# A decoder layer: second norm and feed-forward bias per tile among the gates, projection pieces in column tiles, preparation work spread

## The chip, the cores and the metric

The kernel runs on one core of a Trainium2 chip. The metric is the device time of one execution in microseconds (us). The kernel before was timed three times: 2485.95, 2486.40 and 2489.06 us, median 2486.4. A core has five engines with their own instruction queues, each strictly in order for our purpose: TensorE (PE; its weight loads are listed apart as PEld), VectorE (DVE), ScalarE (ACT), GpSimd (POOL) and SyncE (SP), which here only issues DMAs.

## The reference

One decoder layer in float32 on x of shape 4 x 1024 x 512 (batch, token, feature):

```python
x = layernorm(x + attn(x))          # 32 heads of 16; q, k, v each through two linear layers
x = layernorm(x + gates(x, ctx))    # a causal convolution of two taps, then a gated cell
x = layernorm(x + ffn(x))           # 8 bit quantised input, weights -1, 0, 1, bias

# attn: q = lin(lin(x, wq), vq), the same for k and v; softmax(q k / 4) v; lin(o, wo)
# gates: out = ctx + conv(x) + bias, split in four along 2048 channels (it, ot, gt, ft)
#   ct = sigmoid(ft) * previous_c + sigmoid(it) * tanh(gt);  ht = sigmoid(ot) * tanh(ct)
#   the result is ht and ct, one after the other
# ffn: clip(round(x / scale), -127, 127) * scale, times (ternary_weight - 1), + bias
```

In the gates the tokens of a batch are the channels (1024 = 512 of h and 512 of c) and the 512 features are the sequence.

## The kernel before, in words

**Attention** (`attention`, to line 723). A unit is four heads of one batch, 32 units in all, `u`. Each unit has two passes over its scores: `nat` (L449) computes them with queries in the partitions, and DVE takes their maximum (L465, negated), which is written as a row into the operands of the second pass; `scores` (L519) computes them again, transposed, ACT takes the exponentials (L530), and `weigh` (L545) multiplies by v. `nat` of unit u + 1 runs along with `scores` of unit u. These matmuls contract over 32 rows, so four of them stand in the array side by side as row tiles (the profile writes 32*128); the weighing has 32 output rows for each head, and four heads stand as column tiles (128*32).

The loop runs over 32 steps `h`. Each step issues one `nat` and one `scores`; on every fourth (h % 4 == 1) comes one weighing, on every fourth (h % 4 == 3) one piece of `fill` (or of `out_pieces`): a projection of q or k of a later pair of units in 176 or 160 columns (`project`, L383), a piece of v (`project_v`, L408) or of the output projection (`out_piece`, through `Handed.project`, L222) in 256 columns. These pieces use the full array (128*128): four matmuls that add up over 512 features. A float32 matmul shows as two records. Ahead of the first unit twelve q and k pieces and five `fold_v` pieces (L398) stand next to each other; the last unit has 16 steps without `nat`, with a weighing and an out piece on every second one.

Four `stages` normalise a unit's output: read the denominators (`den`), take reciprocals (L578), spread them (`rbc`), multiply on POOL (`o_n`, L592) and write to HBM. They run at steps 5, 9, 13 and 20 of the next unit. All order in the kernel is the order in which the instructions are written; nothing reorders them within an engine.

Some work for the tail is issued from within: at unit 24, step 5, the loads of the out weights and of the rest (`load_rest`); at step 21 `prepare_rest` turns the ternary weights into floats (L204, POOL) and makes the quantisation scale (L208 to L214, DVE); at unit 30, step 5, `first_norm(0)` begins with `norm_stats` (means L98, square root L107 on ACT, reciprocal L108).

**Tail** (`tail`). A small planner holds later work: `after(n, work)` puts it at the end of the n-th `step()` from there. There is one step for each gate, each out projection tile and each feed-forward tile. Two rounds, for batches (0, 2) and (1, 3). A round has 4 token tiles x 2 batches x 4 gates. A gate (`gate`) is 32 matmuls of 171 columns (64 records; `pc` for two taps, `pa` for two, L792), then four DVE operations (L796 to L802) that add them to the ctx tile `u`, and an ACT function (L803). The convolution uses a fast scheme over three columns, which needs the sum and the difference of the two weight taps (`sum_taps`, L161, POOL) and sums of x (`fir_parts`, L176 to L182, DVE, into `xf`). After a tile's four gates `combine` does six operations on POOL and a Tanh on ACT (L814 to L822), and two bn_stats on DVE (L826, L827). PSUM has two buffers each for `pc`, `pa`, the feed-forward's sum and the transposes.

`second_norm` then normalises a whole batch (L98, L107, L108, L116). Feed-forward takes 16 tiles a round: `quantise` (ACT L862, DVE L863, L864), `turn` (four transposes L870, ACT copy L872), `feed` (L878), `ff_bias` (L909), `residual` (L883, L884), and `third_norm` in groups with the write of the output. `quantise` runs three tiles ahead, `turn` one. Between the rounds `project_out` does the out projection of batches 1 and 3 (L222, 512 columns).

Of the kernel before, what the change touches and what calls it, by code (L numbers as in the profile page):

```python
# [29 lines left out]
def decoder_kernel(ctx: ExitStack, tc: tile.TileContext, a, out):  # L30
# [18 lines left out]
    with ExitStack() as rest:  # L49
        tail(rest, tc, a, out, ident, eps, hand)  # L50


class Handed:
# [47 lines left out]
    def deviations(self, mv, pool, name, t0=0, n=NT):  # L101

        nc = self.nc
        rstd = pool.tile(
            [P, NT], F32, tag="rstd", bufs=1 if pool is self.shared else 3, name=f"rstd{name}_{t0}"
        )
        nc.scalar.activation(rstd[:, t0 : t0 + n], mv[:, t0 : t0 + n, 1], AF.Sqrt, bias=self.eps, scale=1.0)  # L107
        nc.vector.reciprocal(rstd[:, t0 : t0 + n], rstd[:, t0 : t0 + n])  # L108
        return rstd

    def norm_stats(self, stats, pool, name):
        mv = self.means(stats, pool, name)
        return mv, self.deviations(mv, pool, name)
# [6 lines left out]
    def first_norm(self, b):  # L120
# [3 lines left out]

        def deviations():
            made.extend(self.norm_stats(self.stats[b], self.shared, f"1_{b}"))

        def part(t0):
            if t0 == 0:
                self.nc.vector.tensor_copy(x1[:, :, 0], self.z0[:, b, :])  # L130
            for t in (t0, t0 + 1):
                self.normalised(x1[:, t, 1 : D + 1], self.y[b][:, t, :], *made, t)

        return x1, [deviations] + [lambda t0=t0: part(t0) for t0 in range(0, NT, 2)]

    def load_ctx(self, k, pool):
# [4 lines left out]
        u = (pool if k % 2 else self.shared).tile([P, 4, D + 1], F32, tag="u", name=f"u{b}_{t}")  # L141
# [16 lines left out]
    def sum_taps(self, w):  # L158
        for tap, op in ((2, ALU.add), (3, ALU.subtract)):
            for i in range(FT):  # L160
                self.nc.gpsimd.tensor_tensor(w[:, i, tap, :], w[:, i, 0, :], w[:, i, 1, :], op)  # L161
# [39 lines left out]

    def prepare_rest(self):
        nc = self.nc
        nc.gpsimd.tensor_scalar_add(self.w_f, self.w_f.bitcast(mybir.dt.int32), -1.0)  # L204
# [12 lines left out]
    def project(self, b, t, cols, pt, bias=False):  # L217
# [3 lines left out]
        for f in range(FT):  # L221
            nc.tensor.matmul(  # L222
                pt, attn_t[:, f, t * P : (t + 1) * P], self.w_o[:, f, cols], start=f == 0, stop=f == FT - 1
            )
# [8 lines left out]
def attention(ctx, tc, a, attn_d, ident, shared, hand):  # L233
# [8 lines left out]
    b_v = const.tile([P, D], F32, tag="b_v", name="b_v")  # L242
# [37 lines left out]
    for i in range(2):  # L280
        t = once.tile([P, 32], F32, tag=f"neg{i}", name=f"neg{i}")
        nc.gpsimd.memset(t, 0.0)
        negs.append(t)
    for i in range(2):
# [734 lines left out]
```

## Time and profile before

| what | value |
|---|---|
| median of the runs shown | 2486.4 us |
| profiled execution, its own time | 2487.75 us |
| its span, first to last instruction | 2486.0 us |
| mean granted TensorE clock | 0.996 |
| attention, to the first gate | 1974.58 us |
| first gates and feed-forward, to the first out projection | to 2203.64 us |
| second gates | from 2258.57 us |
| last feed-forward matmul, last DVE instruction | about 2478.3, 2482.97 us |

The page gives each engine's busy time, the chain of work that ended last (followed backward from the last instruction through whatever released each step), and groups of instructions by line with their mean time. A line in order of time reads: start, duration, engine, line and operation, output <- input, shape, count of records, and in brackets the engine's idle time before it with what ended it. Idle time of an engine costs only where the chain passes through it.

### The profile page before, as it was taken

What the parts mean: (1) busy time and instruction counts of PE and PEld (TensorE: products, weight loads), DVE (VectorE), ACT (ScalarE), POOL (GpSimd) and SP (SyncE); (2) the same over time, 40 slices, a digit from 0 to 9 for tenths busy, and PEclk for the clock granted to TensorE, in tenths of its full rate; (3) what the DMA queues carried; (4) which work ended last, traced back from release to release, by engine and by line L of the source; (5) the groups of instructions that cost most, each with busy time, mean ns of one, the idle gap of its engine ahead of it and who ended that gap; (6) DMA issues with size and microseconds to landing.
All of it is one profiled execution on the core that took longest, in us unless ns stands there. A gap on an engine that the chain in (4) does not pass through costs nothing.

```text
span 2486.0 us, 60152 instructions
## 1 busy us (share of the span) xinstructions
PE 2452.5 (99%) x25492; PEld 1781.1 (72%) x25492; DVE 1748.6 (70%) x2198; ACT 1306.5 (53%) x2558; POOL 333.5 (13%) x275
## 2 busy tenths in 40 slices
PE   9999999999999999999999999999999999999998
PEld 6677777777777777777777776677776799547984
DVE  3767777777777777777777777777777465888568
ACT  1166666666666666666666666666655511411132
POOL 2000000000000000000000002000020265311640
PEclk9999999999999999999999999999999999999999
DMA  6101111111110211101111114110120243240311
GB/s 216 48 11 20 20 25 54 21 23 22 23 26 16 58 21 20 21 20 23 22 21 21 24 20 134 21 24 16 25 79 11 66 157 136 84 153 18 119 35 68
DMA packets 80653, 120.80 MB, mean 49 GB/s; under 512 B 39056, under 2 KB 39056, under 8 KB 80384
## 3 DMA queue, kind: packets, MB, share of 16 engines
q1 hardware_dynamic: 79808, 115.90, 16.5%
q8 instruction: 201, 3.29, 0.6%
q10 hardware_dynamic: 576, 1.05, 0.1%
q14 instruction: 68, 0.56, 0.1%
HBM read 80.77 MB, written 18.35 MB: 40 GB/s over the span
## 4 chain that ended last, share of the span: by engine, by line
PE 91%; DVE 5%; POOL 2%; DMA 0%; ACT 0%; issue 0%; SPq 0%; DVEq 0%; POOLq 0%
PE nat L449 22%; PE av L545 19%; PE st L519 18%; PE proj L383 10%; PE v L408 5%; PE po L222 5%; PE pa L792 5%; PE pc L792 5%; PE fold L344 1%; PE pf L878 1%; POOL w L161 1%; DVE y L116 1%; DVE y L883 1%; DVE y L909 1%; DVE xq L864 1%; DVE stats L884 1%
## 5 line engine op out<-in xcount | busy, mean ns | idle before, releaser
L465 DVE TENSOR_REDUCE mx<-nat 128x2 f32<-128x1024 f32 x1008 | 1187.7, 1219 | 453.2 <-PE st L519 424.4
L530 ACT ACTIVATE at<-st 128x512 f32<-128x512 f32 x2016 | 1042.4, 603 | 625.5 <-PE st L519 610.0
L449 PE MATMUL nat<-qk 32*128 32x512 f32 x4032 | 1013.3, 614 | 3.8 <-DVE mx L465 3.8
L519 PE MATMUL st<-qk 32*128 32x256 f32 x8064 | 999.2, 387 | 0.0
L519 PEld LDWEIGHTS st<-qk 32*128 32x128 f32 x8064 | 656.0, 184 | 45.7 <-issue 3.1
L545 PE MATMUL av<-at,v_sb 128*32 128x256 f32 x8192 | 498.8, 382 | 0.6 <-ACT at L530 0.6
L449 PEld LDWEIGHTS nat<-qk 32*128 32x128 f32 x4032 | 343.3, 184 | 174.1 <-DVE mx L465 120.3
L545 PEld LDWEIGHTS av<-at,v_sb 128*32 128x32 f32 x8192 | 241.3, 110 | 223.4 <-ACT at L530 90.5
L592 POOL TENSOR_TENSOR o_n<-o_sb,rbc 128x512 f32<-128x512 f32 x64 | 96.1, 1523 | 1694.3 <-DMA rbc<-rec_d 1233.9
L383 PE MATMUL proj<-xT,w_qk 128*128 128x176 f32 (+1 forms) x1536 | 270.2, 320 | 0.7 <-ACT w_qk L349 0.7
L383 PEld LDWEIGHTS proj<-xT,w_qk 128*128 128x128 f32 x1536 | 223.7, 189 | 64.6 <-ACT at L530 60.0
L792 PE MATMUL pc<-xf,w 128*128 128x171 f32 x1024 | 161.9, 310 | 6.0 <-DVE u L796 4.4
L792 PE MATMUL pa<-xf,w 128*128 128x171 f32 x1024 | 161.4, 310 | 0.0
L792 PEld LDWEIGHTS pc<-xf,w 128*128 128x128 f32 x1024 | 153.6, 191 | 7.7 <-DVE u L796 4.9
L792 PEld LDWEIGHTS pa<-xf,w 128*128 128x128 f32 x1024 | 153.7, 191 | 0.0
L803 ACT ACTIVATE u<-u,b_c 128x512 f32<-128x512 f32 x64 | 45.5, 720 | 170.7 <-DVE u L802 170.7
L408 PE MATMUL v<-w_v,xT 128*128 128x256 f32 x512 | 126.0, 391 | 0.0
L222 PE MATMUL po<-w_o,big 128*128 128x256 f32 (+1 forms) x384 | 118.9, 459 | 2.1 <-ACT at L530 2.1
L878 PE MATMUL pf<-w_f,xq_t 128*128 128x512 f32 x256 | 117.2, 602 | 3.8 <-DVE y L883 2.3
L408 PEld LDWEIGHTS v<-w_v,xT 128*128 128x128 f32 x512 | 92.5, 189 | 34.4 <-ACT at L530 16.6
L222 PEld LDWEIGHTS po<-w_o,big 128*128 128x128 f32 x384 | 70.3, 190 | 49.2 <-issue 31.6
L558 DVE TENSOR_TENSOR o_sb<-av,o_sb 128x256 f32<-128x256 f32 x128 | 54.3, 424 | 72.0 <-PE av L545 71.5
(97 smaller groups left out, 1213.2 us busy)
## 6 DMA issues: line engine op xcount, KB each, us to landing
qk<-qk SPq DMA_DIRECT2D x256, 64.0 KB
w<-in_conv_wT SPq DMA_DIRECT2D x32, 512.0 KB
u<-in_ctx SPq DMA_DIRECT2D x16, 1024.0 KB
xT<-in_xT SPq DMA_DIRECT2D x16, 512.0 KB
rbc<-rec_d SPq DMA_DIRECT2D x128, 64.0 KB
attn<-o_n SPq DMA_DIRECT2D x256, 32.0 KB
big<-attn SPq DMA_DIRECT2D x4, 2048.0 KB
y<-in_x SPq DMA_DIRECT2D x4, 2048.0 KB
```

The lines of the kernel that those rows point to most:

```text
L222: nc.tensor.matmul(pt, attn_t[:, f, t * P : (t + 1) * P], self.w_o[:, f, cols], start=f == 0, stop=f == FT - 1)
L383: nc.tensor.matmul(pt[:, 0:n], w[:, f, gg * P : (gg + 1) * P], xts[b][:, f, cols], start=f == 0, stop=f == FT - 1)
L408: nc.tensor.matmul(pt, xts[b][:, f, t * P : (t + 1) * P], w_v[:, f, cols], start=f == 0, stop=f == FT - 1)
L449: nc.tensor.matmul(pts[n], q_ts[u % 4][r : r + 32, qt * P : (qt + 1) * P], k_ts[u % 4][r : r + 32, kh * 512 : kh * 512 + 512], start=True, ...
L465: nc.vector.tensor_reduce(mxs[u][:, qt, 2 * pair : 2 * pair + 2, kh], pt, AX.X, ALU.max, negate=True)
L519: nc.tensor.matmul(st[:, k * QW : k * QW + QW], k_ts[u % 4][r : r + 32, kt * P : (kt + 1) * P], q_ts[u % 4][r : r + 32, qq * QW : qq * QW ...
L530: nc.scalar.activation(at, st, AF.Exp, scale=0.25)
L545: nc.tensor.matmul(av[32 * j : 32 * j + 32, :], v_sb[b % 2][:, kt, c * VW : c * VW + 32], ats[u, 2 * i + n // 2, j][:, n % 2 * QW : n % 2 ...
L558: nc.vector.tensor_add(o, av, o)
L592: nc.gpsimd.tensor_mul(o_n[:, :, half * 256 : half * 256 + 256], o_sb[:, cols].rearrange("p (s e) -> p e s", e=2), rbc[:, cols].rearrange( ...
L792: nc.tensor.matmul(pt, w[:, i, tap, o : o + P], xf[:, tap, i, :], start=i == 0, stop=i == FT - 1)
L878: nc.tensor.matmul(pt, xq_ts[b, t][:, f, :], hand.w_f[:, f, :], start=f == 0, stop=f == FT - 1)
```

## The change

1. `by_quarters`: the q, k, v, fold and out pieces of attention are issued as four column tiles of 32 output rows each, for each of the four contraction steps (16 matmuls where there were 4). The out projection in the tail stays as it was.
2. `prepare_w_f` in four parts at step 21 of units 25 to 28; the scale at step 21 of unit 29 (`prepare_rest`).
3. `first_norm` has its means apart from its square root, and the reciprocal is issued with the first normalised part. At unit 30 only the means are issued; the parts of the last unit begin a step earlier. At the end of attention the last unit's reciprocals stand between the two halves of `first_norm(2)`.
4. The sums of weights come in quarters, after steps 3, 6, 6 and 7; those for the second round at its start.
5. The second norm is done for each pair of tiles (h and c) in `combine`, as steps 3 to 6; the last of them adds the feed-forward's bias on POOL, into the place of x1 that is no longer needed. `residual` adds from there; `ff_bias` and `second_norm` go. The first three tiles are quantised after the first three of the last four gates.
6. Feed-forward goes through the tiles in the order 0, 1, 2, 4, 5, 6, 3, 7; its very last tile is done in two halves of 256 columns; statistics are kept in order of work; the third norm's groups and their steps differ.
7. Memory: ctx tiles share two slots in `shared`, both loaded in the last unit; `rbc` has a pool of its own; `b_v` shares the slot of `b_f`; batch 3's attention is loaded after step 9 of the first feed-forward in place of step 1.

```diff
+def by_quarters(nc, pt, lhsT, rhs):
+    for f in range(FT):
+        for j in range(4):
+            r = slice(32 * j, 32 * j + 32)
+            nc.tensor.matmul(pt[r, :], lhsT(f)[:, r], rhs(f), start=f == 0, stop=f == FT - 1)
...
     def deviations(self, mv, pool, name, t0=0, n=NT):
...
-        nc.scalar.activation(rstd[:, t0 : t0 + n], mv[:, t0 : t0 + n, 1], AF.Sqrt, bias=self.eps, scale=1.0)
-        nc.vector.reciprocal(rstd[:, t0 : t0 + n], rstd[:, t0 : t0 + n])
-        return rstd
+        part = rstd[:, t0 : t0 + n]
+        nc.scalar.activation(part, mv[:, t0 : t0 + n, 1], AF.Sqrt, bias=self.eps, scale=1.0)
+        return rstd, lambda: nc.vector.reciprocal(part, part)
...
-    def sum_taps(self, w):
+    def sum_taps(self, w, i):
         for tap, op in ((2, ALU.add), (3, ALU.subtract)):
-            for i in range(FT):
-                self.nc.gpsimd.tensor_tensor(w[:, i, tap, :], w[:, i, 0, :], w[:, i, 1, :], op)
+            self.nc.gpsimd.tensor_tensor(w[:, i, tap, :], w[:, i, 0, :], w[:, i, 1, :], op)
...
+    def prepare_w_f(self, f):
+        w = self.w_f[:, f, :]
+        self.nc.gpsimd.tensor_scalar_add(w, w.bitcast(mybir.dt.int32), -1.0)
...
         pt = ps_st.tile([P, QW], F32, tag="st", name=f"proj{p}_{which}_{t0}")
-        for f in range(FT):
-            nc.tensor.matmul(
-                pt[:, 0:n], w[:, f, gg * P : (gg + 1) * P], xts[b][:, f, cols], start=f == 0, stop=f == FT - 1
-            )
+        by_quarters(nc, pt[:, 0:n], lambda f: w[:, f, gg * P : (gg + 1) * P], lambda f: xts[b][:, f, cols])
...
-                if u >= 0 and i > 2 and firsts:
+                if u >= 0 and i > 1 and firsts:
                     firsts.pop(0)()
...
-                if i == 3 and u >= 0:
-                    hand.load_ctx(0, None)
-                if i == 10 and u >= 0:
-                    hand.sum_taps(hand.first_w)
+                if i in (3, 5) and u >= 0:
+                    hand.load_ctx(i // 2 - 1)
+                if i in (8, 9, 10, 11) and u >= 0:
+                    hand.sum_taps(hand.first_w, i - 8)
...
-                if h == 21 and u == 24:
+                if h == 21 and 25 <= u < 29:
+                    hand.prepare_w_f(u - 25)
+                if h == 21 and u == 29:
                     hand.prepare_rest()
...
     hand.x1[2], parts = hand.first_norm(2)
-    for part in parts:
+    for part in parts[:2]:
+        part()
+    stages.pop(0)()
+    for part in parts[2:]:
         part()
...
+    def combine(b, t, k):
+        u, y, x = us[b, t], ys2[b], x1[b]
         ig, og, gg, fg = (u[:, i, 0:D] for i in range(4))
+        both = (t, 4 + t)
+        made = []
...
         def third():
-            nc.vector.bn_stats(stats2[b][:, 4 + t, :], y[:, 4 + t, :])
-            nc.vector.bn_stats(stats2[b][:, t, :], y[:, t, :])
-        after(2 if last else 1, second)
-        after(4 if last else 3, third)
...
+            for n, tt in enumerate(both):
+                nc.vector.bn_stats(stats2[b][:, 2 * t + n, :], y[:, tt, :])
+            made.append(hand.means(stats2[b], stat, f"2_{b}", 2 * t, 2))
+        def fourth():
+            made.extend(hand.deviations(made[0], stat, f"2_{b}", 2 * t, 2))
+        def fifth():
+            mv, rstd, invert = made
+            invert()
+            for n, tt in enumerate(both):
+                hand.normalised(y[:, tt, :], y[:, tt, :], mv, rstd, 2 * t + n)
+        def sixth():
+            for tt in both:
+                nc.gpsimd.tensor_add(x[:, tt, 0:D], y[:, tt, :], b_f)
+        for n, work in ((1, second), (3, third), (4, fourth), (5, fifth), (6, sixth)):
+            after(n, work)
...
+    def residual(b, n, t, pt, cols=slice(0, D), half=0):
+        x2 = ys2[b][:, t, cols]
+        nc.vector.tensor_add(x2, pt, x1[b][:, t, cols])
+        nc.vector.bn_stats(stats3[b][:, n + half, :], x2)
...
+            if (b, n) == (B - 1, NT - 1):
+                for half in range(2):
+                    cols = slice(half * 256, half * 256 + 256)
+                    pt = feed(b, t, cols)
+                    residual(b, n, t, pt, cols, half)
...
+            group = {5: 2, 6: 1, 7: 1}.get(n, 4 if n == 3 else 0) if last else 4 * (n % 4 == 3)
             if group:
-                third_norm(b, t + 1 - group, group, end > 3)
+                first, invert, parts = third_norm(b, n + 1 - group, group)
+                first()
+                if group == 4:
+                    after(1, invert)
+                    for m, part in enumerate(parts):
+                        after(1 + m, part)
...
-                    gate(b, t, g, w, (lambda: [turn(batches[0], tt) for tt in (0, 1)]) if last else None)
+                    gate(b, t, g, w, (lambda: [turn(batches[0], order[m]) for m in (0, 1)]) if last else None)
                     if g == 3:
-                        combine(b, t, k, last)
-                        if t == 3 and b == batches[0]:
-                            after(3, lambda b=b: second_norm(b, True))
+                        combine(b, t, k)
+                    if t == 3 and b == batches[1] and g < 3:
+                        quantise(batches[0], order[g])
                     if b == batches[0] and g == 0 and (n, t) != (1, 3):
                         w_next = hand.load_conv(4 * n + t + 1, wp)
-                        after(3, lambda w=w_next: hand.sum_taps(w))
+                        if t < 3:
+                            for i, m in enumerate((3, 6, 6, 7)):
+                                after(m, lambda w=w_next, i=i: hand.sum_taps(w, i))
...
-            after(1, lambda: hand.load_attention(3, hand.shared.tile([P, NT * (D + 1)], F32, tag="big0", name="big3")))
+            after(9, lambda: hand.load_attention(3, big3()))
```

## The prediction

> **What bounds the kernel.** I read the page's engine shares first, then the chain that ended last, then the order of time in the places where the chain leaves TensorE.
>
> ```profile
> PE 2452.5 (99%) x25492; PEld 1781.1 (72%) x25492; DVE 1748.6 (70%) x2198; ACT 1306.5 (53%) x2558; POOL 333.5 (13%) x275
> PE 91%; DVE 5%; POOL 2%; DMA 0%; ACT 0%; issue 0%; SPq 0%; DVEq 0%; POOLq 0%
> ```
>
> TensorE is busy 99% and is 91% of the chain. So time is won in two ways only: TensorE's own work gets shorter, or one of its few waits goes. For the first, the order of time on TensorE in a steady attention unit:
>
> ```profile
> 624.55 1.93 PE L545 MATMUL av<-at,v_sb 128*32 128x256 f32 x32
> 626.42 0.70 PE L449 MATMUL nat<-qk 32*128 32x512 f32 x2
> ...
> 628.35 1.99 PE L408 MATMUL v<-w_v,xT 128*128 128x256 f32 x8
> 630.28 0.70 PE L449 MATMUL nat<-qk 32*128 32x512 f32 x2
> ```
>
> Both pieces stream 256 columns eight times (a float32 matmul is two records). The weighing, in four column tiles (128*32), takes 626.42 - 624.55 = 1.87 us from its start to the next block's; the full-array piece takes 1.93. At single records it is 1.864 and 1.924. The difference is at the head: the first weights take 186 ns to load for 128 columns, 106 for 32, and the second pass starts 320 ns after the first in a v piece, 240 in a weighing. The quarters give 20 ns back, since the fourth starts 20 ns after the first.
>
> The waits, in order of time:
>
> ```profile
> 1546.56 5.38 POOL L204 TENSOR_SCALAR w_f<-w_f 128x2048 f32<-128x2048 int32 x1
> 1546.91 3.31 DVE L213 TENSOR_TENSOR sc<-sc 128x1 f32<-128x1 f32 x1
> 1551.47 0.70 PE L449 MATMUL nat<-qk 32*128 32x512 f32 x2 [3.35 <-DVE mx L465]
> 1877.34 1.99 PE L222 MATMUL po<-w_o,big 128*128 128x256 f32 x8 [2.12 <-ACT at L530]
> 1990.74 2.60 PE L792 MATMUL pc<-xf,w 128*128 128x171 f32 x16 [1.89 <-DVE u L796]
> 2016.83 4.24 PE L792 MATMUL pc<-xf,w 128*128 128x171 f32 x16 [2.50 <-DVE u L796]
> 2131.05 0.66 PE L870 MATMUL tr<-ident,xq 128*128 128x128 f32 x4 [2.64 <-DVE xq L864]
> 2142.36 0.63 PE L870 MATMUL tr<-ident,xq 128*128 128x128 f32 x4 [2.37 <-DVE xq L864]
> ```
>
> The brackets are TensorE's idle time. 4.24 us for 16 records that take 2.5 elsewhere is half the clock. The view by stretches (TensorE, its loads, DVE, ACT, POOL; the last three are granted clock, DMA share, GB/s) has it after the first gap too:
>
> ```profile
> 1550.00:1612.00 62.00, 60.53 (x716) 42.61 (x720) 44.51 (x48) 37.04 (x74) 4.89 (x3) 0.97 0.11 21
> ```
>
> 0.97 of 62 us is 3.4 us at half, at most 1.7 us lost; so after the gaps of 3.35, 2.50, 2.64 and 2.37, not after 2.12.
>
> **A. Quarters.** Between two row-tiled blocks stand 178 projection pieces, 58 of v, 25 of out and one fold, each with the same head: 262 x 0.060 = 15.7 us. Seven further out pieces of the last unit follow a weighing directly; both become column tiles, and the change of tiling between them (about 0.09 us of spacing and 0.10 of exposed weight load) goes: 7 x 0.20 = 1.4. The pieces ahead of the first unit stand next to each other and gain nothing. **17.1 us**, all on the path, since each unit repeats at 57.84 us with DVE at 71% and ACT at 64%. Below: 13, if a third of the head stays with 160 and 176 columns, which no column tile of the trace has.
>
> A rule of the Trainium skill speaks against it ("TensorE: Matmul & The Clock Gate", the section on 56 against 53.3 ns): a matmul has an issue floor of about 25 ns, or about 62 ns when the instructions are decoded by the sequencer. Four quarters at 62 are 248 ns a pass, where a projection's pass takes 150 (176 columns) or 136 (160): some 150 us lost over all pieces. The weighing's row decides: four records a pass of 216 ns, 54 each, so 62 does not hold here. The 25 would cost nothing (4 x 25 is under 136). The trace shows single starts 7 ns apart but no sustained rate under 54 ns; the pieces need 34 to 37. I take the floor as not binding; the rest is a rival below.
>
> **B. Preparation of the rest.** The outputs' spacing shows the loss in that unit: v at 1503.66, which plus 57.84 minus 7.65 (the pair's distance) is 1553.85, and the piece comes at 1559.14: 5.29 us. The cause is DVE's scale operations (1x1 tensor-tensor, 0.14 us alone, up to 3.31 beside GpSimd's 5.38), with eight reductions queued behind. Now GpSimd's operation is four of some 1.35 us, one per unit, and the scale is made at unit 29, step 21. There GpSimd's adds and o_n end at 1835.5, and step 21 falls at about 1839, so seven operations cost DVE some 1.1 us, against slack of about 1.4 per reduction pair. I take 0.3 us left: **5.0** (3 to 5.3).
>
> **C. First norm at unit 30.** Table load 1.28, sqrt 0.30, table load 1.28 hold ACT 2.9 us and DVE's reciprocal 1.92. They move to the last unit, step 2, where ACT waits anyway (weighing and out piece give 3.6 us of TensorE work in between): **2.1** (0 to 2.1).
>
> **D. Start of the tail to the end of the first feed-forward**: 1974.58 to 2203.64 = 229.1 us. TensorE's own work: 32 gates x 4.67 = 149.3, two turns 0.9, feed-forward 14 x 3.87 + 2 x 3.44 = 61.1. The excess is 17.8. What goes: the 1.89 (rbc has its own pool, so the new xf no longer waits for o_n), the 2.50 with its slow clock (DVE's L827 waited for POOL behind eight sums of taps, 9.92 us; they come in quarters after steps 3, 6, 6, 7, so combine starts with its gate), and the 6 us in which feed-forward was DVE's (4.1 to 4.8 us a tile; minus the 0.69 of ff_bias and the second norm's 0.5, under 3.87). GpSimd gets 2 x 1.2 more per tile pair: 2 x (7.1 + 2.4) + 10 = 29 of 37.3 us, which fits.
>
> What comes: reciprocal L578 now stands ahead of the eight L116, and den lands about 1.5 us after its last issue (as rec_d does), so DVE is 2.7 us later; the third gate's PSUM needs it only at 1984.0, covered by 1.3 us. In the last four gates each quantise waits behind its gate's ACT (0.72 + 0.81), and stands ahead of DVE's next gate. Following the queues from gate 4's end: DVE 2.0, first xq 6.1 (GpSimd beside it stretches L863/L864 to 1.3 each, as at 2140), gate 5 done 8.6, second xq 11.0, bn_stats 12.4, gate 6 14.9, its ACT and identity 16.4, sqrt with a table load 18.0, copies of the transposes from there: the first feed has its operand at 18.6, where TensorE is at 14.9. Without the stretch it is 1.8 us late. I take 2.8, and 1.0 for the clock. The Tanh of the last combine stands ahead of the fourth quantise (second is no longer put off): another 2.2. New: 149.3 + 0.9 + 2.8 + 1.0 + 61.1 + 2.2 = 217.3, gain **11.8** (5 to 17).
>
> Here a second rule weighs: "ScalarE: Activation LUTs", what a table load costs: 1283 ns and a drain of 1380 for each switch. The trace has 1.28 and 0.30, and the next load at once, 2.9 a pair. Sixteen norms now switch among the gates; at 2.9 a pair stays inside a gate's 4.67 us. At the page's 5.3 it would not, and the copies at both ends would be 1.4 later: 2.8 us in all. I take the row.
>
> **E. Second round**: gates from 2258.57, last feed until 2478.26 = 219.7. It waited less (0.97 from xf, 0.71 and 0.2 at the turn). New: 217.3 + 0.97 = 218.2: **1.5** (-4 to 6.5).
>
> **F. The end**: from the last matmul to the span's end 7.7 us, 2 of them DVE's lag. New: half an add 0.43, stats 0.4, means 0.2, sqrt and reciprocal 0.8, L116 0.55, write 3.0 = 5.5: **2.2** (1 to 3).
>
> **At nothing**, and what hides it: the second ctx tile's 1 MB leaves at step 5 of the last unit, not on SP ahead of the weights' issue at 1992.24 (gain up to 0.4 in a queue with 20 us to spare; without it SP's den, rec and rbc of unit 30 come 0.4 later). Batch 3's attention (2 MB) leaves SP nine tiles into feed-forward, not at its first, since its slot is now read until tile 8; it is needed 60 us later, and a late one would stop the output writes behind it on SP. b_f takes b_v's slot; its load at unit 24 finds v's last add (unit 23) done. The weights' sums for round two move from POOL among the gates to the 55 us of the out projection.
>
> **Sum**: 17.1 + 5.0 + 2.1 + 11.8 + 1.5 + 2.2 = 39.7. The profiled execution took 2487.75 us with a span of 2486.0; the median shown is 2486.4, 1.35 below it. Taken from the median: **2446.7 us**.
>
> **Rivals.** *Quarters gain nothing* (short passes expose their weights): 22.6 left, 2464. *The tail's waits only move* (D and E give nothing, new waits at the turn as long as the old): 39.7 - 13.3 = 26.4, 2460. For it: my queue walk finds 6 us of new waits a round. Against: the feed-forward's DVE lag goes anyway. *Slower: issue bound.* If a matmul can't follow another column tile faster than every 54 ns, every projection pass takes 216: 119 x 8 x 66 + 59 x 8 x 80 ns = 101 us lost; 2486.4 - 22.6 + 101 - 15.7 = 2549. It decides from about 43 ns on, where quarters lose the 22.6 won elsewhere. For it: no sustained rate under 54 in the trace. Against: starts 7 ns apart, 1.7 us of "issue" waits ahead of L545 in 8192 loads.
>
> **Numbers.** Both parts work: 0.73, own range 2436 to 2458. Quarters nothing 0.10; tail nothing 0.09; slower 0.06; parts that cancel to within 0.2% (5 us, about what this measurement can tell) 0.02. 80% range: the best ends (17.1, 5.3, 2.1, 17, 6.5, 3) give 2435, the worst with quarters at 13 (3, 0, 5, -4, 1) 2468. So 2434 to 2468; faster 0.92, same 0.02, slower 0.06.
>
> **What would show it.** A unit's repeat falls from 57.84 to 57.36 us; v pieces take 1.864 from start to next block, projections 1.33; no wait of TensorE at 1548 or 1875; nothing behind POOL in the first round; feed-forward at 3.87 a tile; a wait of 2 to 4 us at each turn. Wrong if projections take 1.39 or more, or if the turns grow to over 10 us.

## The result

The changed kernel takes 2455.66 us (median of four runs, 2454.71 to 2456.35); the kernel before takes 2486.98 (2485.95 to 2489.06). The ratio is 0.9873, 95% interval 0.9856 to 0.989: 31.3 us faster, where 39.7 were forecast. The profiled executions differ by a little more, 33.0 (2487.75 and 2454.71; spans 2486.0 and 2452.9), because the one of before lies 0.8 above its median and the one of after 0.95 below. The account by stages is made from these two spans.

| stage of the span, us | before | forecast | after | run 10 |
|---|---|---|---|---|
| start to the first gate | 1974.6 | 1950.4 | 1951.1 | 1951.5 |
| gates, round one | 162.0 | 150.2 | 150.5 | 151.3 |
| wait between last gate and first feed | 0 | 2.8 | 3.7 | 0 |
| feed-forward, round one | 67.1 | 64.3 | 66.7 | 63.1 |
| out projection | 54.9 | 54.9 | 54.9 | 54.9 |
| gates, round two | 152.2 | 151.2 | 151.6 | 151.6 |
| wait between last gate and first feed | 0.7 | 2.8 | 3.7 | 0 |
| feed-forward, round two | 67.0 | 64.3 | 64.0 | 61.7 |
| last matmul to the end | 7.7 | 5.5 | 6.75 | 6.8 |

The forecast column is what the prediction's steps give for each stage; its 1.0 us for the clock and its 2.2 for the Tanh stand in feed-forward here. The last column belongs to run 10 below, the fastest version. The turn is the change from gates to feed-forward. In the kernel before, its waits of 2.64 and 0.20 us lie ahead of the transposes inside the last gate, so they stand in the row of the gates.

Attention came out 0.7 us over the forecast and the gates 0.3 and 0.4. Most of the shortfall lies behind the gates: 0.9 in each turn, 2.4 in feed-forward of round one and 1.25 at the end.

### The profile page after: what moved, and what is told of

Its sections match the earlier page's. It is cut to its first block, busy times and chain, and to the rows that moved or that the text cites. A ratio compares the mean times of both kernels' runs of the same rounds, so it can differ in the third digit from the quotient of the medians.

```text
span 2452.9 us, 74387 instructions
## 1 busy us (share of the span) xinstructions
PE 2431.9 (99%) x32604; PEld 1691.8 (69%) x32604; DVE 1736.9 (71%) x2180; ACT 1337.4 (55%) x2592; POOL 373.7 (15%) x310
## 4 chain that ended last, share of the span: by engine, by line
PE 97%; DVE 2%; ACT 1%; issue 0%; DVEq 0%
PE nat L457 22%; PE av L553 20%; PE st L527 18%; PE proj L59 10%; PE pa L802 5%; PE pc L802 5%; PE v L59 5%; PE pf L884 4%; PE po L59 2%; PE po L237 2%; PE fold L361 1%; PE fold L59 1%; PE tr L876 0%; DVE xq L869 0%; DVE y L121 0%; DVE xq L870 0%
## 5 line engine op out<-in xcount | busy, mean ns | idle before, releaser
L59 PE MATMUL proj<-xT,w_qk 128*32 128x176 f32 (+1 forms) x6144 | 259.4, 311 | 0.7 <-ACT w_qk L366 0.7
L59 PEld LDWEIGHTS proj<-xT,w_qk 128*32 128x32 f32 x6144 | 181.3, 109 | 82.0 <-ACT at L538 60.0
L884 PE MATMUL pf<-w_f,xq_t 128*128 128x512 f32 (+1 forms) x264 | 120.8, 604 | 7.6 <-ACT xq_t L878 7.6
L59 PE MATMUL v<-w_v,xT 128*32 128x256 f32 x2048 | 122.5, 382 | 0.0
L59 PEld LDWEIGHTS v<-w_v,xT 128*32 128x32 f32 x2048 | 60.6, 109 | 58.1 <-ACT at L538 16.6
L170 POOL TENSOR_TENSOR w<-w 128x512 f32<-128x512 f32 x64 | 80.5, 1292 | 110.5 <-DMA w<-in_conv_wT 110.5
L564 ACT COPY o_sb<-av 128x256 f32<-128x256 f32 x128 | 48.0, 375 | 77.9 <-PE av L553 59.3
```

The lines of the kernel that those rows point to most:

```text
L59: nc.tensor.matmul(pt[r, :], lhsT(f)[:, r], rhs(f), start=f == 0, stop=f == FT - 1)
L884: nc.tensor.matmul(pt, xq_ts[b, t][:, f, :], hand.w_f[:, f, cols], start=f == 0, stop=f == FT - 1)
```

## The profile after

The page's engine shares and the chain that ended last, of the changed kernel:

```profile
PE 2431.9 (99%) x32604; PEld 1691.8 (69%) x32604; DVE 1736.9 (71%) x2180; ACT 1337.4 (55%) x2592; POOL 373.7 (15%) x310
PE 97%; DVE 2%; ACT 1%; issue 0%; DVEq 0%
```

TensorE has 7112 more matmul records and 20.6 us less busy time; its share of the chain rose from 91% to 97%, and POOL has left the chain. "issue" stays at 0%: the added instructions hold nobody up.

TensorE in order of time in a steady unit (start, time, engine, line, operation, shape):

```profile
622.89 1.93 PE L59 MATMUL v<-w_v,xT 128*32 128x256 f32 x32
624.76 0.70 PE L457 MATMUL nat<-qk 32*128 32x512 f32 x2
...
638.09 1.40 PE L59 MATMUL proj<-xT,w_qk 128*32 128x176 f32 x32
639.42 0.70 PE L457 MATMUL nat<-qk 32*128 32x512 f32 x2
...
680.25 1.93 PE L59 MATMUL v<-w_v,xT 128*32 128x256 f32 x32
```

From a piece's start to the next block's is now 1.87 us for v (1.864 at single records, before 1.924) and 1.33 for a projection of 176 columns (1.331, before 1.391; 160 columns went from 1.284 to 1.224). The busy numbers mislead: 1.93 against 1.99 is the same 0.06, but they overlap the next block. The same v piece returns after 680.25 - 622.89 = 57.36 us, the forecast to the last digit.

The stretch in which the kernel before lost 5.3 us to the preparation, by the view of stretches (TensorE, its loads, DVE, ACT, POOL, then granted clock, DMA share, GB/s):

```profile
1502.00:1564.00 62.00, 62.00 (x984) 42.21 (x976) 45.00 (x48) 40.18 (x82) 12.11 (x11) 1.00 0.41 131
1800.00:1862.00 62.00, 62.00 (x910) 39.57 (x906) 48.83 (x69) 35.21 (x70) 12.84 (x10) 1.00 0.07 17
```

TensorE is busy through all 62.00 us at clock 1.00. The second line is the stretch in which the scale is made now (from 1821.5; its seven operations take 0.15 to 0.16 us each): no loss there either. What is left of the first norm's cost, moved to the last unit, and then TensorE around the first turn into feed-forward (a gate is 16 matmuls, so 32 records, 16 of `pc` and 16 of `pa`; the description ahead of the prediction gives twice that):

```profile
1915.35 2.32 PE L553 MATMUL av<-at,v_sb 128*32 128x256 f32 x29 [0.89 <-ACT at L538]
...
2099.03 2.50 PE L802 MATMUL pa<-xf,w 128*128 128x171 f32 x16
2105.23 6.57 PE L884 MATMUL pf<-w_f,xq_t 128*128 128x512 f32 x8 [3.70 <-ACT xq_t L878]
2111.64 0.60 PE L876 MATMUL tr<-ident,xq 128*128 128x128 f32 x4
2112.07 3.60 PE L884 MATMUL pf<-w_f,xq_t 128*128 128x512 f32 x8
...
2136.07 0.63 PE L876 MATMUL tr<-ident,xq 128*128 128x128 f32 x4 [1.03 <-DVE xq L870]
2136.67 3.67 PE L884 MATMUL pf<-w_f,xq_t 128*128 128x512 f32 x8
2140.64 0.63 PE L876 MATMUL tr<-ident,xq 128*128 128x128 f32 x4 [0.30 <-DVE xq L870]
```

The first feed waits 3.70 us for its operand, and its eight records then take 6.57 in place of 3.60: half the clock, 3.0 us more for this tile. What that costs the whole is a matter of run 4. The feed-forward's later waits of 1.03 and 0.30 (a third of 0.24 follows) were not in the forecast. ScalarE, POOL and DVE in these stretches show what they stand behind:

```profile
2101.67 0.72 ACT L813 ACTIVATE u<-u,b_c 128x512 f32<-128x512 f32 x1 [4.86 <-DVE u L812]
2102.30 0.80 ACT L868 ACTIVATE xq<-y,magic,sc 128x512 f32<-128x512 f32 x1
2103.11 1.28 ACT L117 ACT_TABLE_LOAD   x1
2104.41 0.29 ACT L117 ACTIVATE rstd<-mv,eps 128x2 f32<-128x2 f32 x1
2104.61 1.05 ACT L878 COPY xq_t<-tr 128x512 f32<-128x512 f32 x2
```

```profile
2125.87 2.91 POOL L855 TENSOR_TENSOR big<-y,b_f 128x512 f32<-128x512 f32 x2 [9.05 <-DVE y L121]
2128.75 10.94 POOL L170 TENSOR_TENSOR w<-w 128x512 f32<-128x512 f32 x8
```

```profile
2133.04 1.48 DVE L869 TENSOR_SCALAR xq<-xq 128x512 f32<-128x512 f32 x1
2134.55 1.37 DVE L870 TENSOR_SCALAR xq<-xq,sc 128x512 f32<-128x512 f32 x1
```

The copies that turn the first two tiles (L878) stand behind a gate's function, a quantise, a table load and a square root. And the sums of weights for round two (L170), which the prediction put into the 55 us of the out projection, run from 2128.75 to 2139.69, in the middle of feed-forward (the out projection begins at 2171.9). Beside them the two quantising operations ahead of the wait of 1.03 take 1.48 and 1.37 us, where they take 0.42 and 0.49 from 2142.19 on, with POOL idle.

## The experiments

Times are medians against the kernel before on the same chip, which took 2485.05 to 2485.71 there, up to 1.9 us less than beside the changed kernel (2486.98). So two medians of different occasions are not compared to the last microsecond; where one is said to be slower or faster by a few, the stages of the two profiles are the evidence.

**1. Quarters alone.** The kernel before with the pieces between scores in column tiles and nothing else of the change.

```diff
-        for f in range(FT):
-            nc.tensor.matmul(pt, xts[b][:, f, t * P : (t + 1) * P], w_v[:, f, cols], start=f == 0, stop=f == FT - 1)
+        by_quarters(nc, pt, lambda f: xts[b][:, f, t * P : (t + 1) * P], lambda f: w_v[:, f, cols])
...
```

> The kernel before, with its q, k, v, fold and out pieces in four column tiles and nothing else. Theory (the gain lies at the head of each piece that follows a change of tiling): 262 pieces x 0.060 us and some 1.4 us in the last unit, so about 17 us less than before, 2470; v pieces 1.864 us from start to the next block, projections 1.331 and 1.224; the waits at 1551, 1877, 2017, 2131 and 2142 stay as they were. Rival (the quarters bring nothing, the waits do): no difference from before. Rival (issue bound): slower, projections over 1.39 us.

Measured: 2472.41, ratio 0.9944 (0.9929 to 0.9959). The pieces took 1.864, 1.331 and 1.224 us to the next block. Attention fell by 15.3 us, not 17.1, with the wait for the preparation still in it and longer:

```profile
1539.35 1.22 PE L450 MATMUL nat<-qk 32*128 32x512 f32 x2 [3.98 <-DVE mx L466]
```

3.98 is 0.63 more than before, and 6.8 us of half clock followed where it was 3.4 before, up to 1.7 more. With these the pieces' own gain is 15.3 + 0.6 + 1.7 = 17.6 at most. Of the other waits, expected to stay as they were, the one ahead of the first turn grew from 2.64 to 4.75. What follows: step A holds in size, and "quarters gain nothing" falls.

**2. Two column tiles of 64 in place of four of 32**, in the changed kernel.

```diff
-        for j in range(4):
-            r = slice(32 * j, 32 * j + 32)
+        for j in range(2):
+            r = slice(64 * j, 64 * j + 64)
```

> The changed kernel with two column tiles of 64 rows each in place of four of 32. Theory (what is saved is the time to load the first weights, 186 ns for 128 columns and 106 for 32, so about 133 for 64, less 7 ns for each further tile): a v piece takes about 1.878 us from start to the next block, 0.014 more than in quarters, and the time rises by 262 x 0.014 = 3.7 us, to 2459. Rival (any column tiling saves the same, since it spares a part of the change of tiling): pieces at 1.864, no change of the time. Rival (only 32 wide tiles help, the kind of the weighing beside it): pieces at 1.924, 16 us more, 2472.

Measured: 2458.67 (0.9889, 0.9874 to 0.9903). A piece of v:

```profile
623.90 1.95 PE L59 MATMUL v<-w_v,xT 128*64 128x256 f32 x16
625.77 0.70 PE L457 MATMUL nat<-qk 32*128 32x512 f32 x2
```

At single records pieces took 1.878, 1.344 and 1.237, each 0.013 to 0.014 longer, and attention 1954.93, 3.9 longer; 262 x 0.014 = 3.7. So the gain is the head of each piece, a size that grows with the columns of the first weight load (186 ns for 128 columns, 133 for 64, 106 for 32). The passes' rate has no part in it: behind the first pass they follow every 216, 149 and 136 ns in all three versions.

**3. The scale apart from the weights' conversion**, in the kernel before: the conversion on GpSimd goes to unit 26 whole, DVE's seven small operations stay at unit 24.

```diff
     def prepare_rest(self):
...
-        nc.gpsimd.tensor_scalar_add(self.w_f, self.w_f.bitcast(mybir.dt.int32), -1.0)
...
+                if h == 21 and u == 26:
+                    hand.prepare_w_f()
```

> The kernel before, with the conversion of the ternary weights on GpSimd, whole, two units later (unit 26, step 21), while the scale on VectorE stays at unit 24. Theory (the two stood in each other's way, the size of the one operation did not matter): the wait of 3.35 us at 1551 goes and none appears at unit 26, 4 to 5 us less than before, 2482. Rival (a GpSimd operation of 5.38 us holds VectorE's other work too, so that only the split helps): a wait of some 3 us in unit 26, no gain.

Measured: 2483.09 (0.999, 0.9983 to 0.9997; twenty runs), 2.6 us less than before, where 4 to 5 were expected. The wait of 3.35 became 0.40, and none came at unit 26. Attention is 3.0 shorter; a stretch of 3.4 us at half clock fell elsewhere in that execution, so the clock's share of step B does not show in it. What follows: the wait came from the two standing side by side, not from the conversion's 5.38 us as such. What the clock behind that wait is worth over many runs is not shown.

**4. Idle matmuls ahead of each feed-forward**, in the changed kernel. Nobody reads their result.

```diff
         closing = []
+        warm = ps_o.tile([P, D], F32, tag="o", name=f"warm{batches[0]}")
+        for _ in range(4):
+            nc.tensor.matmul(warm, ident, hand.w_f[:, 0, :], start=True, stop=True)
```

> The changed kernel with four matmuls of 512 columns, whose sum nobody reads, ahead of each feed-forward, so that TensorE isn't idle in its wait of 3.70 us there. Theory (the idle time costs a second time by the granted clock: the first feed-forward tile takes 6.57 us in place of 3.60): the first feed still starts at the same time, the tile takes 3.6, 3.0 us less in each round, 2449.7. Rival (the slow first tile comes from something else, its operands or the PSUM): no change, or up to 0.5 us more for the four matmuls.

Measured: 2456.04 (0.9877, 0.9863 to 0.9892), a miss by 6.3. TensorE at the turn:

```profile
2100.36 2.50 PE L802 MATMUL pa<-xf,w 128*128 128x171 f32 x16
2102.70 3.59 PE L923 MATMUL warm<-w_f,ident 128*128 128x512 f32 x8
2106.55 3.70 PE L884 MATMUL pf<-w_f,xq_t 128*128 128x512 f32 x8 [0.25 <-ACT xq_t L878]
...
2115.83 0.66 PE L876 MATMUL tr<-ident,xq 128*128 128x128 f32 x4 [1.71 <-DVE xq L870]
```

The clock was kept: the first tile takes 3.70. But the first feed starts no earlier after the last gate, and the third turn now waits 1.71 (1.73 in round two). The third turn, here and in the expectations, is the fourth tile's: the first two tiles are turned together inside the last gate. So the slow clock was not on a path of its own: beside it lay a second chain, that of the fourth tile's quantise, which ends about as late. In this chain, by the lines of the changed kernel: the last gate's function (2106.97), two POOL operations (L829, L830; the third, L828, is done by then), the Tanh of the last combine, the fourth tile's identity, DVE's two operations, the turn:

```profile
2106.97 0.72 ACT L813 ACTIVATE u<-u,b_c 128x512 f32<-128x512 f32 x1
2110.41 0.63 ACT L833 ACTIVATE u<-u 128x512 f32<-128x512 f32 x1 [2.72 <-POOL u L830]
2110.95 0.80 ACT L868 ACTIVATE xq<-y,magic,sc 128x512 f32<-128x512 f32 x1
```

Another trace shows this without any matmul added. In run 7, whose code is that of the changed kernel up to here, the half clock did not come in round one:

```profile
2105.55 3.70 PE L884 MATMUL pf<-w_f,xq_t 128*128 128x512 f32 x8 [3.68 <-ACT xq_t L878]
...
2114.92 0.63 PE L876 MATMUL tr<-ident,xq 128*128 128x128 f32 x4 [1.80 <-DVE xq L870]
```

Feed-forward of round one took 66.50 us in it, against 66.69 with 6.8 us of half clock: there the slow clock cost 0.2 (0.4 in round two, by 64.02 against 63.58 with the clock full in run 4). In runs 2, 4, 6, 7 and 11 the third turn starts 12.9 to 13.1 us after the last gate's end in both rounds, whether the first feed starts 2.1 or 3.7 us after it, and whether the clock is full or halved for 3.4 us. In the changed kernel's profile, with 6.8 us at half, it is 14.0 and 13.8.

**5. The first three tiles quantised earlier**, among the gates of the batch before.

```diff
-                    if t == 3 and b == batches[1] and g < 3:
+                    if t == 3 and b == batches[0] and g < 3:
```

> The changed kernel with the first three tiles quantised among the first batch's last gates, four gates earlier. Theory now (after the run with idle matmuls: two waits follow each other at the turn, the copies of the transposes, 3.70 us, and then the fourth tile's operand, which comes through the last gate's ACT, POOL, Tanh, quantise; the later one sets the time): VectorE no longer lags at the turn, so the last gate's ACT comes some 3 us earlier, the wait of 3.70 us goes, and one of about 2 us stays ahead of the third turn; 3 to 4.5 us less in each round, 2448. Rival (the first wait sets the time, with its clock): 6.7 us less in each round, 2442. Rival (the later chain doesn't move with it): no gain, 2455.

Measured: 2449.74 (0.9855, 0.9841 to 0.987). Both waits of 3.70 and the half clock behind them are gone, 13 us in all; 5.9 of it reach the time, a little under the 3 to 4.5 expected for each round, since the third turn shows the second chain again (with some half clock behind its wait in round one, 1.08 for the transposes in place of 0.60):

```profile
2103.28 3.60 PE L884 MATMUL pf<-w_f,xq_t 128*128 128x512 f32 x8
...
2113.07 1.08 PE L876 MATMUL tr<-ident,xq 128*128 128x128 f32 x4 [2.31 <-DVE xq L870]
```

**6. The square root later.** The later parts of the first batch's last combine go one step later, so that its table load stands behind the copies.

```diff
...
-        for n, work in ((1, second), (3, third), (4, fourth), (5, fifth), (6, sixth)):
+        for n, work in ((1, second), (3, third), (4 + late, fourth), (5 + late, fifth), (6 + late, sixth)):
...
-                        combine(b, t, k)
+                        combine(b, t, k, int(t == 3 and b == batches[0]))
```

> The changed kernel with the first batch's last square root (table load 1.28 and 0.30 us) one step later, behind the copies of the transposes. Theory (the later chain sets the time): the wait at the turn falls from 3.70 to about 2.1 us, but the fourth tile's operand comes no earlier, so the time changes by less than 1 us, 2455. Rival (the first wait sets the time): 1.6 us and a part of the slow clock less in each round, 2451 or under.

Measured: 2458.70 (0.9891, 0.9876 to 0.9906), 3.0 slower than the changed kernel, a miss. The first feed did come earlier (a wait of 2.11), but the third turn came no earlier, 12.9 us after the last gate: it waits 1.56, and 3.28 in round two. So the wait that the profile shows ahead of the first feed was not the one that sets the time. The table loads now stand between the last gate's function and the Tanh, but put the Tanh off by under 0.1 us (8.95 after the last gate, 8.88 in the changed kernel), since POOL is not done sooner. What is new is the fourth turn's wait of 0.96 in each round. By the order on DVE, the normalisation that moved along now stands ahead of the fifth tile's quantise; this was not tested apart:

```profile
2116.99 1.00 DVE L121 TENSOR_SCALAR y<-y,mv,rstd 128x512 f32<-128x512 f32 x2
2117.90 1.48 DVE L869 TENSOR_SCALAR xq<-xq 128x512 f32<-128x512 f32 x1
```

**7. The sums of weights issued later**, after steps 3 to 6 of the out projection.

```diff
-            for i in range(FT):
-                hand.sum_taps(w_next, i)
+            for i in range(FT):
+                after(3 + i, lambda i=i: hand.sum_taps(w_next, i))
```

> The changed kernel with the sums of the second round's first weights put at the ends of steps 3 to 6 of the out projection in place of its start. Theory (in the changed kernel GpSimd has nothing ahead of them in its queue and does them in the first feed-forward, at 2128.75 to 2139.7, where they stretch VectorE's operations from 0.4 to 0.5 us to 1.4): the waits of 1.03, 0.30 and 0.24 us at 2136 to 2146 go, up to 1.6 us less, 2454. Rival (they come from the bias adds or from the third norm's group): they stay.

Measured: 2454.93 (0.9879, 0.9862 to 0.9895), and no effect on what it was to move:

```profile
2128.86 10.95 POOL L170 TENSOR_TENSOR w<-w 128x512 f32<-128x512 f32 x8
```

Same place, same length. The operation stands later in the program, but POOL's queue is empty of anything that waits ahead of it, so it runs when POOL is free. This run tells nothing of the cause of the waits at 2136.

**8. Runs 5 to 7 together, with quantising four tiles ahead** instead of three (and as many more buffers for it).

```diff
...
-                    if t == 3 and b == batches[1] and g < 3:
+                    if t == 3 and b == batches[0]:
...
-                if k + 3 < len(tiles):
-                    quantise(tiles[k + 3][0], tiles[k + 3][2])
+                if k + 4 < len(tiles):
+                    quantise(tiles[k + 4][0], tiles[k + 4][2])
```

> The changed kernel with all three edits, and with quantising four tiles ahead in place of three, the first four among the first batch's last gates (five buffers for xq, three for its transpose). Theory: no wait over 0.5 us is left at either turn or in feed-forward; the first round's feed-forward takes 61.5 us in place of 66.7, the second's 61.5 in place of 64.0, and the two waits of 3.70 go: some 15 us less than the changed kernel, 2441. If the third turn's operand is still late, 2445 to 2448.

Measured: 2459.90 (0.9896, 0.9882 to 0.9911), a miss by 19. TensorE, and DVE ahead of its first wait:

```profile
2094.53 4.27 PE L802 MATMUL pc<-xf,w 128*128 128x171 f32 x16 [2.68 <-DVE u L806]
2116.79 3.67 PE L884 MATMUL pf<-w_f,xq_t 128*128 128x512 f32 x8 [2.38 <-DVE y L889]
```

```profile
2089.94 1.38 DVE L870 TENSOR_SCALAR xq<-xq,sc 128x512 f32<-128x512 f32 x1
2091.42 2.52 DVE L121 TENSOR_SCALAR y<-y,mv,rstd 128x512 f32<-128x512 f32 x2
2093.87 0.61 DVE L806 TENSOR_TENSOR u<-pc,u 128x342 f32<-128x342 f32 x1
```

A fourth quantise and a normalisation stand between two gates on DVE, both stretched (0.49 and 1.00 elsewhere), and the gate's PSUM is freed too late. The run changes four things at once; which of them makes the feed-forward's new waits on L889 it doesn't tell.

**9. Run 5, with the whole of the last combine one step later.** The fourth tile's identity then stands ahead of the last Tanh.

```diff
...
-            after(n, work)
+            after(n + late, work)
...
-                        combine(b, t, k)
+                        combine(b, t, k, int(t == 3 and b == batches[1]))
```

> The changed kernel with the quantising of the first three tiles one gate group earlier (as in the run before that took both 3.70 waits away) and all later parts of the last combine of a round one step later, so that the identity of the fourth feed-forward tile stands ahead of that combine's Tanh on ScalarE. Theory (a second chain, last gate's function, three POOL operations, Tanh, identity of the fourth tile, DVE's two operations, holds the third turn): the 2.3 us of the third turn go in both rounds; 2449.7 - 2 x 2.3 = 2445, within 1.5. Rival (the feed-forward is held by DVE and ScalarE as such, so that a wait only moves to the next tile): within 1.5 of 2449.7, with a new wait of 1.5 us or more at the fourth or fifth turn.

Measured: 2446.69 (0.9845, 0.9831 to 0.986), just outside the 1.5 around 2445. The third turn no longer waits in either round. Feed-forward of round two, which has no sums of weights, is 61.69 us against 64.01 in run 5, so there the second chain set the time and no wait took its place. In round one the waits around the sums grew instead, so there waits did move, with half the clock behind the last of them (four records in 3.63):

```profile
2130.99 0.63 PE L876 MATMUL tr<-ident,xq 128*128 128x128 f32 x4 [0.87 <-DVE xq L870]
2136.45 0.63 PE L876 MATMUL tr<-ident,xq 128*128 128x128 f32 x4 [1.19 <-DVE xq L870]
2141.01 0.63 PE L876 MATMUL tr<-ident,xq 128*128 128x128 f32 x4 [0.29 <-DVE xq L870]
2143.33 3.63 PE L884 MATMUL pf<-w_f,xq_t 128*128 128x512 f32 x4 [1.69 <-ACT xq_t L878]
```

**10. Run 9, with the sums of weights for round two among the gates**, as the kernel before had them.

```diff
...
-            for i in range(FT):
-                hand.sum_taps(w_next, i)
...
-                        if t < 3:
-                            for i, m in enumerate((3, 6, 6, 7)):
-                                after(m, lambda w=w_next, i=i: hand.sum_taps(w, i))
+                        for i, m in enumerate((3, 6, 6, 7)):
+                            after(m, lambda w=w_next, i=i: hand.sum_taps(w, i))
```

> The kernel of the run beside it, with the sums of weights for round two again among the gates of the last token tile of round one, not ahead of the out projection. Theory (POOL runs these sums at once, so they lie in the first feed-forward, where they stretch DVE's small operations and cause its waits of 1.03, 0.30 and 0.24 us): these waits go, 1 to 1.5 us under the run beside it, if POOL's sums among the gates do not reach the turn; the operation on w leaves the stretch from 2128 to 2140 us. Rival (the waits come from the order of DVE's own work): no difference in these waits, or 1 to 3 us slower since POOL now delays the last gates' combine.

Measured: 2442.14 (2441.59 to 2442.49; ratio 0.9826, 0.981 to 0.9842), 4.5 less than run 9 where 1 to 1.5 were expected: in run 9 these waits had grown to 4.0 us with some half clock behind them. It is the fastest version. All four waits went, and one of 0.57 came. POOL does the sums beside the last gates:

```profile
2096.02 2.52 POOL L855 TENSOR_TENSOR big<-y,b_f 128x512 f32<-128x512 f32 x2
2098.48 7.47 POOL L170 TENSOR_TENSOR w<-w 128x512 f32<-128x512 f32 x6
2105.89 1.29 POOL L828 TENSOR_TENSOR u<-u 128x512 f32<-128x512 f32 x1
```

Gates take 151.34 us (151.30 in run 9), feed-forward of round one 63.06 (68.13). So it was the sums that made the waits of run 9, for the bias adds (2.91 us from 2127.34) and the third norm's group stay in feed-forward and no such wait comes with them. POOL does delay the last combine now, as the rival said: its Tanh comes 7.2 us after the last gate in place of 5.5. It costs next to nothing, since by run 9's order nothing of the fourth tile waits for that combine any more.

**11. The last feed-forward tile whole**, in the changed kernel.

```diff
...
-                for half in range(2):
-                    cols = slice(half * 256, half * 256 + 256)
+                for half in range(1):
+                    cols = slice(0, D)
```

> The changed kernel with the last feed-forward tile whole, as it was before the change, not in two halves. If the halves shorten the end as the prediction has it, the stretch from TensorE's last matmul to the span's end grows from 6.75 us by 0.5 to 0.7 (whole add and statistics, 1.3, against 0.83 for the second half). If VectorE is held until after the last matmul by the two normalisations ahead (as the trace of the changed kernel suggests), the first half gains nothing and the stretch stays within 0.2 of 6.75, or gets shorter.

Measured: from the last matmul to the end 6.51 us, against 6.74 to 6.76 in every trace with halves. Feed-forward of round two does not change: 63.55, against 63.58 to 63.59 with halves in runs 2, 4 and 7 (the 64.02 of the changed kernel's profile has 6.8 us of half clock in it). One run took 2453.43; a difference of 2 us between single executions is no verdict, but the stretch is clear. DVE's order at the end of the changed kernel says why:

```profile
2446.00 1.00 DVE L121 TENSOR_SCALAR y<-y,mv,rstd 128x512 f32<-128x512 f32 x2
2446.91 0.42 DVE L889 TENSOR_TENSOR y<-pf,big 128x256 f32<-128x256 f32 x1
```

TensorE ends at 2446.17. The first half's add, which was to run before that, comes at 2446.91, behind two normalisations.

## Why the prediction was right, and where it was wrong

The sign, the mechanism of attention and the range were right; the time came out 9 us later than forecast. By spans the gain is 33.0 for 39.7, and the steps account for the 6.7:

**A (17.1) held.** Pieces measure as forecast (1.864 and 1.33), run 1 gives the size, and run 2 its cause. The issue floor of about 62 ns for a matmul decoded by the sequencer (the Trainium skill, "TensorE: Matmul & The Clock Gate", the section on 56 against 53.3 ns), which the prediction had set against the weighing's 54 ns, does not show here: a projection of 160 columns issues four matmuls a pass and keeps a pass of 136 ns, 34 ns each on average. This also closes the slower rival, which decided from 43 ns. The 54 was no limit: it is the pass of 256 columns, 216 ns, divided by four.

**B (5.0) held for the wait**: 62.00 of 62.00 us busy, and 3.35 us of waiting gone. The rest of the 5.0, the clock's part, is not shown apart: run 3 took away the same wait alone, and over twenty runs that gave 2.6 us (0.7 to 4.2). **C (2.1) was mis-sized by 0.9**: in the last unit the table loads still hold the exponentials, and a weighing waits 0.89 at 1915.35, where I had 3.6 us of cover. That the loads make this wait is read from the order on ScalarE and was not tested apart. A, B and C together are 23.5 for 24.2.

**D (11.8) gave 8.0.** In us over the forecast: gates 0.3; the turn 0.9; feed-forward 2.4; the kernel before was 0.2 shorter here than the 229.1 of the sum.

The turn was mis-sized. The walk through the queues had found the operand at 18.6 and TensorE at 14.9, a wait of 3.7, and the trace has 3.70. I then took 2.8, between this and the 1.8 of a walk without the stretch by GpSimd; for the first quantise, where the walk has it, the stretch was there in full:

```profile
2090.08 1.39 DVE L869 TENSOR_SCALAR xq<-xq 128x512 f32<-128x512 f32 x1 [1.50 <-ACT xq L868]
2091.50 1.37 DVE L870 TENSOR_SCALAR xq<-xq,sc 128x512 f32<-128x512 f32 x1
```

In feed-forward, the clock's 1.0 and the Tanh's 2.2 were added, but are not two terms of a sum: the Tanh lies on a second chain beside the turn's wait and its slow clock, and the longer one counts. In the profiled execution the clock took 3.0 and the third turn waited for nothing; with the clock full (run 7) the third turn waited 1.80 and the round was 0.2 shorter. That 3.2 was forecast for a stretch that cost 3.0 is luck. What is left, 2.6, is the error of "At nothing": the sums of weights were moved in the program to the out projection, but not in time, and stretch DVE in feed-forward. By runs 9 and 10 this costs 4.5 us once the other waits are gone; in the changed kernel it was not measured apart. The price of the norms among the gates held: a table load, the square root and the load back take 2.89 us (2079.94 to 2082.83), as the row had it.

**E (1.5) gave 0.5**: gates 0.4 and the turn 0.9 over the forecast, feed-forward 0.3 under. The wait of 0.96 for xf stayed, as the step said. Its list of the waits of before left out one of 2.32 at 2417.34; the sum, which builds on D, does not need it. **F (2.2) gave 0.95**: its items add up to 5.4, not 5.5, and leave out the first half of the last tile. The halves were to hide an add and its statistics behind TensorE, but DVE came to the first half 0.74 us after TensorE's end and spent 0.80 on it; run 11 shows that the halves gain nothing and cost 0.24.

The rival "the tail's waits only move" (2460) is nearer to the measured 2455.7 than the forecast itself (2446.7), but not for its reason: of 13.3 us in D and E, of which it gives nothing, 8.5 came. With the edits of runs 5, 9 and 10 the change reaches 2442.1, below the forecast.

## What to carry to other kernels

A wait with a slow clock behind it and a later wait on another chain are not two terms of a sum: follow each chain to the instruction that it delays, and count the longer. Work without a wait in its queue runs as soon as its engine is free, wherever the program puts it, so "moved to a later stage" is a claim on the queue and has to be read there. And when a walk through the queues gives one number with the stretch seen in the nearest row of a trace and a smaller one without, here the row's was right: 3.7 for 3.70.

## What the runs showed of the hardware that was not expected

- Matmuls in four column tiles kept one in 34 ns on average over a whole piece of 160 columns: four start within 20 ns, and the next four 136 ns after the first four. The trace of before had shown 54, in the weighing.
- The half clock came after gaps of 1.7 to 4.75 us, for 3.4 or 6.8 us at a time, and not the same in every execution of the same code: the wait of 3.7 us at the first turn was followed by 6.8 us of it in the changed kernel, 3.4 in run 11 and none in run 7. Where it came for 6.8, the tile behind the gap took 3.0 and 2.8 us more in the two rounds, of which 0.2 and 0.4 reached their length. Four idle matmuls in the gap took it away.
- With GpSimd at work beside them, DVE's quantising operations of 128x512 took 1.27 to 1.52 us in place of 0.42 and 0.49, and two normalisations 2.52 in place of 1.00. The adds that read one operand from PSUM (0.68) and the statistics (0.70) kept their length beside it (2130.40 and 2131.11, next to the sums of weights).
